# Contexts of the last block combined from SBUF, the choice of tokens marked on logits, unused products on TensorE, and six groups of weights ahead

## The chip, the core and the metric

The kernel runs on one core of one Trainium2 chip. The metric is the device time of one execution in microseconds. Times of a kernel agree within about 0.3% from run to run.

## What is computed

An image batch x of shape (4, 64, 64, 128) goes through two layers. In what follows L = 4096 is the number of tokens of an image, C = 128 the channels.

Layer 0 normalises x by groups and adds a selective scan over the tokens in three directions. Layer 1 works on the tokens of each image, and its code is what the change touches:

```python
t = t + attn(ln(t))          # q = products of cosines, 16 heads of 8 channels, softmax(q q^T / sqrt(8)) q
#   attn: x1 = ln(x + ctx @ w_comb.T + b_comb);  zf = cos(x1[:, :8]) * cos(ry)
#         ln(x1 + relu(zf @ w1.T + b1) @ w2.T + b2)
t = t + experts(ln(t))
#   experts: probs = softmax(x @ gate_w.T + gate_b, over the tokens)      64 experts
#            per expert the 8 tokens of highest probability: pooled = sum(prob * token)
#            out = gelu(pooled @ weight1 + bias) @ weight2 + bias
#            each of the 8 tokens receives prob * out
```

So each expert reads and writes 8 of the 4096 tokens of an image; the softmax over the tokens needs the logits of the whole image.

## The kernel before

Everything runs on the one core, in an order that is written out by hand: the instructions of each engine execute in the order in which the program emits them (`manual_schedule`), and pieces of work are Python generators that are stepped beside a main loop.

**Attention loop** (`loop`). For one image there are 1024 rounds: 4 sets of heads j, 8 blocks qb of 512 queries (`QB`), 32 chunks kc of 128 keys. A round computes scores on TensorE (L998), their exponential on ScalarE (L1003), and adds the values product into one PSUM bank `acc` (L1012). Row 8 of each head's 32 rows of `acc` holds the sum of the exponentials, because the values carry a column of ones. After 32 rounds `sums` copies `acc` to the tile `av` (L1021; on VectorE for the last image) and stores contexts and sums to memory (L1027, L1030, issued on POOL). For the last image (b = 3) the rounds are sorted by block (`by_block`), so the last 128 rounds are block 7 with j = 0 to 3.

In round i the program emits first the scores of round i + 1, then the step of the work beside it, then the values product of round i. For the last image the work beside is `last.turn(1.5, ...)`: each round adds a credit of 1.5 steps (at most 3 are saved), and at most one step that emits TensorE work is run in a round. A generator says that its next step is TensorE work by yielding `PE`, which `bank.take` does; beside the loop there is one PSUM bank for all of it.

**Work beside the last loop** (`last`, a chain). In this order: what is left of image 2; the experts' biases; for the image pairs (0, 1) and then (2,) `search` (logits in, the 8 highest: L1290, L1292), `choice` and `gather`; then `after` for the blocks 0 to 6 of image 3 as they become whole; then `search` of image 3 over the first seven blocks.

**The end of attention** (`after`). Per block: sums are read, inverted (L1090), stored and read back spread over the 8 channels of each head (L1102); contexts are read (L1100) and multiplied (L1107), combined with `w_comb` (co, L1115), added to the tokens, normalised (`norm`, L878 to L884, with two small operations on POOL), the cosine (Sin on ScalarE, L1226), transposed (zt, L1138), h (L1156), Relu (L1161), fo (L1169), normalised twice, transposed (xT, L1193), logits (lg, L1207, L1211).

**Choice** (`choice`). ScalarE takes the exponential of the 8 highest values (L1312) and of all logits in place (L1316), VectorE replaces the 8 highest by -1 in a copy (`match_replace`, L1320), and one pass over all 4096 columns keeps the probability where the copy is negative and zero elsewhere (L1330). `gather` then takes each group of 512 tokens: wt (chosen tokens transposed and scaled, L1342), a copy (L1348), pool (L1353), an addition (L1359), with the tokens loaded by L1337.

**Experts** (`answers`). 16 groups of 4 experts (`GE`), each with 2.1 MB of weights (L1370, L1373). Five groups are loaded ahead: one during the loop, three after it and one after the last block's logits, both on ScalarE's queue (`prefetch`). The other eleven are loaded on SP as buffers come free; two groups are in flight (`flow(..., 2, 4)`: at most two, the second four steps after the first). Then the answers go through memory (L1458, L1462), and `scatter` adds them to the tokens: 32 tiles of 512 tokens, each loaded on POOL's queue (L1440), added (L1476, L1483) and stored on SP (L1485), in a ring of `DEEP` = 12 tiles.

Of the kernel before, what the change touches and what calls it, by code (L numbers as in the profile page):

```python
# [16 lines left out]
P = 128  # L17
# [16 lines left out]
VJ = 60  # L34
QB = 512
F32R = mybir.dt.float32r


HIGH = 0xFFFFF000
# [674 lines left out]
class Attention:  # L714
# [3 lines left out]
    def __init__(self, tc, ctx, w, gate, cols, ident, bank, dram, t1, w_out, scans, sz, x):  # L718
# [52 lines left out]
        self.small = ctx.enter_context(tc.tile_pool(name="a_small", bufs=2))  # L771
        self.u, self.q, self.v, self.context, self.total, self.t2 = {}, {}, {}, {}, {}, {}
        self.xn, self.logits, self.angled, self.whole, self.closed = {}, {}, {}, {}, {}
        self.lag, self.cut = 0, False
        self.round = column(nc, const, ROUND, "round"), column(nc, const, -ROUND, "minus_round")

# [171 lines left out]
    def loop(self, b, beside, by_block=False):  # L948
# [68 lines left out]

        def sums(j, qb, i):

            av = self.mid.tile([P, QB], F32, tag="av", name=f"av_{b}_{j}_{qb}")  # L1020
            (nc.vector.tensor_copy if by_block else nc.scalar.copy)(av, accs.pop((j, qb)))  # L1021
            cut = slice(qb * QB, (qb + 1) * QB)

            def store():
                for k in range(4):
                    h = 4 * k + j
                    nc.gpsimd.dma_start(  # L1027
                        out=self.context[b][h * D : h * D + D, cut], in_=av[32 * k : 32 * k + D, :]
                    )
                nc.gpsimd.dma_start(  # L1030
                    out=self.total[b][qb].rearrange("(k j) t -> j k t", j=4)[j], in_=av[D::32, :]
                )
                if by_block and j == 3:
                    self.whole[b] = qb + 1

            later[i + 3] = store
# [22 lines left out]
    def after(self, b, gs=range(L // QB), to=None):  # L1059
# [172 lines left out]
        yield from cosines()  # L1232
        yield from flow((second(g) for g in gs), self.n, 32 // self.n)


DEEP = 12


class Experts:
# [4 lines left out]
    def __init__(self, tc, ctx, ident, weight1, weight2, block, nb):  # L1244
        nc = self.nc = tc.nc
        self.tc, self.ident, self.weight1, self.weight2, self.block, self.nb = tc, ident, weight1, weight2, block, nb
        self.const = const = ctx.enter_context(tc.tile_pool(name="e_const", bufs=1, side="right"))
        self.some = ctx.enter_context(tc.tile_pool(name="e_some", bufs=2, side="right"))
        self.bias_2 = const.tile([P, C], F32, name="bias_2")
        for k in range(2):  # L1250
            nc.scalar.dma_start(out=self.bias_2[k * E : (k + 1) * E], in_=weight2[:, FFN, :])
        self.bias_1 = const.tile([P, 4, E], F32, name="bias_1")
        self.chosen = [const.tile([P, L], F32, name=f"chosen_{j}") for j in range(nb // 2)]

        self.pooled = const.tile([P, E, 32], F32, name="pooled")
        nc.gpsimd.memset(self.pooled, 0.0)

        self.share = const.tile([P, nb // 2], F32, name="share")
        self.diagonal = const.tile([P, nb // 2, E], F32, name="diagonal")
        self.found, self.ahead, self.rooms = {}, [], 0  # L1260

    def biases(self):

# [15 lines left out]
    def search(self, images, blocks):  # L1279

        nc = self.nc
        rows = slice(images[0] % 2 * E, images[-1] % 2 * E + E)
        prob = self.const.tile([P, L], F32, tag="prob", name=f"prob_{images[0]}")
        best = self.some.tile([P, TOP + QB], F32, tag="best", bufs=1, name=f"best_{images[0]}")
        self.found[images] = rows, prob, best
        while self.block.closed[images[-1]] < blocks:
            yield WAIT
        for b in images:
            own = slice(b % 2 * E, b % 2 * E + E)
            nc.sync.dma_start(out=prob[own, : blocks * QB], in_=self.block.logits[b][:, : blocks * QB])  # L1290
        yield
        nc.vector.max(out=best[rows, :TOP], in_=prob[rows, : blocks * QB])  # L1292
        yield
# [6 lines left out]
    def choice(self, images, blocks):  # L1300

        nc, some, key = self.nc, self.some, images[0]
        rows, prob, best = self.found[images]
        top = some.tile([P, TOP], F32, tag="top", name=f"top_{key}")[rows]
        if blocks * QB < L:
            nc.vector.max(out=top, in_=best[rows, : TOP + L - blocks * QB])
        else:
            nc.vector.tensor_copy(top, best[rows, :TOP])
        low = some.tile([P, 1], F32, tag="low", name=f"low_{key}")[rows]
        nc.vector.tensor_scalar_mul(low, top[:, 0:1], -1.0)  # L1310
        yield
        nc.scalar.activation(top, top, AF.Exp, bias=low)  # L1312
        total = some.tile([P, NC], F32, tag="total", name=f"total_{key}")[rows]
        for g in range(NC):
            cut = prob[rows, g * T : (g + 1) * T]
            nc.scalar.activation(cut, cut, AF.Exp, bias=low, accum_out=total[:, g : g + 1])  # L1316
            yield

        w = self.chosen[key // 2][rows]
        nc.vector.match_replace(out=w, in_to_replace=top, in_values=prob[rows], imm_value=-1.0)  # L1320
        yield
        share = self.share[rows, key // 2 : key // 2 + 1]
        nc.vector.tensor_reduce(share, total, mybir.AxisListType.X, ALU.add)
        nc.vector.reciprocal(share, share)
        for b in images:
            own = slice(b % 2 * E, b % 2 * E + E)
            nc.vector.tensor_scalar_mul(
                self.diagonal[own, b // 2, :], self.ident[own, own], self.share[own, b // 2 : b // 2 + 1]
            )
        nc.vector.scalar_tensor_tensor(w, w, 0.0, prob[rows], ALU.is_lt, ALU.mult)  # L1330
        yield

    def pool(self, b, g):

        nc, bank, rows = self.nc, self.block.bank, slice(b % 2 * E, b % 2 * E + E)
        x = self.some.tile([P, 4, C], F32, tag="x", bufs=4, name=f"x_{b}_{g}")
        nc.sync.dma_start(out=x, in_=self.block.xn[b][:, g * 4 : g * 4 + 4, :])  # L1337
        yield
        ps = yield from bank.take(f"wt_{b}_{g}")
        for i in range(4):  # L1340
# [8 lines left out]
        bank.leave()  # L1349
        yield  # L1350
        ps = yield from bank.take(f"pool_{b}_{g}")
        for i in range(4):
            nc.tensor.matmul(ps[:, :E], x[:, i, :], wT[:, i, :], start=(i == 0), stop=(i == 3))  # L1353
        yield
        into = self.pooled[:, :, b]
        if g == 0:
# [3 lines left out]
        bank.leave()  # L1360
        yield

    def gather(self, images):
        yield from flow((self.pool(b, g) for b in images for g in range(NT // 4)), 2, 3)

    def weights(self, stream, g, by):

# [58 lines left out]
    def answers(self, ctx, out):  # L1426
        nc, tc, bank, nb = self.nc, self.tc, self.block.bank, self.nb
        once = ctx.enter_context(tc.tile_pool(name="e_once", bufs=1))
        pool = ctx.enter_context(tc.tile_pool(name="e_pool", bufs=2))
        deep = ctx.enter_context(tc.tile_pool(name="e_deep", bufs=DEEP))  # L1430
        ng = E // GE
        n = len(self.ahead)
# [12 lines left out]
        def group(g):  # L1445
            yield from self.answer(g, loaded.pop(g), o_all, pool)
            if g + n < ng:
                loaded[g + n] = self.weights(self.ahead[g % n][1], g + n, nc.sync)
            elif len(ts) < DEEP:
                bring(len(ts))  # L1450

        yield from flow((group(g) for g in range(ng)), 2, 4)
        for i in range(len(ts), DEEP):
            bring(i)
        answers = [once.tile([P, C], F32, name=f"answer_{j}") for j in range(nb // 2)]
# [66 lines left out]
def tile_kernel(tc, ctx, x, in_proj_w, dirs, out_proj_w, attn, gate, weight1, weight2, out):  # L1522
# [81 lines left out]
    scanning.close()  # L1604
    experts = Experts(tc, ctx, ident, weight1, weight2, block, nb)
    experts.prefetch(experts.room(ctx, 1, "right"), nc.gpsimd)
    blocks = L // QB
    pairs = [(b, b + 1) for b in range(0, nb - 2, 2)] + [(nb - 2,), (nb - 1,)]
    with tc.manual_schedule():
# [4 lines left out]
                for part in (experts.search(images, blocks), experts.choice(images, blocks), experts.gather(images))  # L1614
            ),
            block.after(nb - 1, range(0, 4)), block.after(nb - 1, range(4, 6)), block.after(nb - 1, range(6, blocks - 1)),
            experts.search(pairs[-1], blocks - 1),
        )
        block.loop(nb - 1, lambda i: last.turn(1.5, i % 3 > 0 or i > 830), True)
        last.rest()  # L1620
        block.cut = False
    loop.close()
    with ExitStack() as end:
        block.bank = Bank(end.enter_context(tc.tile_pool(name="end_ps", bufs=7, space=PSUM)), 7)
        with tc.manual_schedule():
            room = experts.room(end, 3)
            with ExitStack() as pieces:
                block.pieces_of(pieces, 1, opening=False)
                closing = block.after(nb - 1, range(blocks - 1, blocks), experts.rest(pairs[-1], blocks - 1))
                for i, _ in enumerate(closing):  # L1630
                    if i == 2:
                        experts.prefetch(room, nc.scalar)
            experts.prefetch(experts.room(end, 1), nc.scalar)
            for _ in experts.choice(pairs[-1], blocks - 1):
                pass
            for _ in experts.gather(pairs[-1]):
                pass
            for _ in experts.answers(end, out):
                pass

# [31 lines left out]
```

## Time and profile before

| | us |
|---|---|
| median of three runs | 11418.36 (11410.22 to 11421.47) |
| the profiled execution, its own time | 11412.32 |
| its span | 11410.5 |
| TensorE busy in the span | 9874.3 (87%) |
| ScalarE busy | 9993.7 (88%) |
| VectorE busy | 8258.3 (72%) |
| last product of the attention loop ends | 11161.9 |
| co of the last block starts | 11187.6 |
| its lg starts | 11226.1 |
| first wt of the last image starts | 11246.4 |
| first product of the experts starts | 11281.9 |
| last copy of the experts' outputs ends | 11355.3 |
| first product of scatter starts | 11364.6 |

The lower rows come from the timeline of the profiled execution, which lists the instructions of every engine with their start and duration. Of the 249 us after the attention loop each engine is busy for a part only. In the page's slices of the span TensorE's granted clock is full in most of the attention loops; behind the last one it is half for long stretches.

### The profile page before, as it was taken

How to read it: one execution, taken by the hardware profiler on the slowest of the kernel's cores; microseconds unless marked ns; L12 is line 12 of the kernel's file. 1: busy time of each engine (PE TensorE's matmuls, PEld its weight loads, DVE VectorE, ACT ScalarE, POOL GpSimd, SP SyncE). 2: the span in 40 equal slices, each digit the busy share in tenths (PEclk: the TensorE clock that was granted, in tenths of full speed). 3: DMA queues.
4: the chain of work that ended last, by engine and by line, in shares of the span. 5: the costliest groups of instructions: out<-in, count | busy, mean ns of one | idle time of the engine just before them, and what ended most of it. 6: DMA issues, size and time to landing. Idle time of an engine off the chain costs nothing.

```text
span 11410.5 us, 183033 instructions
## 1 busy us (share of the span) xinstructions
PE 9874.3 (87%) x68358; PEld 3273.6 (29%) x68358; DVE 8258.3 (72%) x8405; ACT 9993.7 (88%) x10828; POOL 3790.3 (33%) x3891
## 2 busy tenths in 40 slices
PE   6687792788998889899998899999998999999995
PEld 2233331222222222222222222222222223333323
DVE  6889997888888987999988979988998321111212
ACT  4566672899999999999999999999999999989992
POOL 4777784332323223424333124243331110000000
PEclk8798895899999999999999999999999999999997
DMA  6778897656565665665656755656556332222225
GB/s 188 226 231 230 226 249 198 161 145 156 142 155 155 178 174 146 158 154 142 151 147 160 194 157 156 156 141 151 146 147 162 116 100 72 76 71 84 75 65 186
DMA packets 900980, 1747.52 MB, mean 153 GB/s; under 512 B 203150, under 2 KB 443846, under 8 KB 899830
## 3 DMA queue, kind: packets, MB, share of 16 engines
q1 hardware_dynamic: 764734, 1469.68, 47.9%
q0 software_dynamic: 93856, 156.41, 4.8%
q10 hardware_dynamic: 41496, 109.71, 3.6%
q8 instruction: 537, 8.80, 0.3%
q14 instruction: 357, 2.92, 0.1%
HBM read 1379.76 MB, written 355.47 MB: 152 GB/s over the span
## 4 chain that ended last, share of the span: by engine, by line
PE 38%; ACT 24%; issue 14%; DVE 11%; DMA 10%; POOL 1%; SPq 1%; ACTq 0%; DVEq 0%; POOLq 0%
PE acc L1012 21%; ACT e L1003 20%; PE s L998 10%; DVE h L561 5%; DMA delta<-d_delta 4%; PE cv L412 2%; DMA du<-d_du 2%; DVE dB L551 1%; ACT dA L542 1%; PE y L599 1%; ACT delta L542 1%; PE fo L1169 1%; PE xd L426 1%; PE h L1156 1%; DMA w<-in_L_ffn_weight_dram 1%
## 5 line engine op out<-in xcount | busy, mean ns | idle before, releaser
L1003 ACT ACTIVATE e<-s 128x1024 f32<-128x1024 f32 x8192 | 7778.1, 1105 | 234.2 <-PE s L998 222.2
L1012 PE MATMUL acc<-e,val 128*32 128x512 f32 x32768 | 5250.2, 615 | 106.5 <-ACT av L1021 93.7
L998 PE MATMUL s<-qm,key 32*128 32x512 f32 x16384 | 2650.8, 501 | 588.8 <-ACT e L1003 558.9
L998 PEld LDWEIGHTS s<-qm,key 32*128 32x128 f32 x16384 | 1013.4, 184 | 4444.4 <-issue 2483.9
L563 POOL COPY ends<-h 128x1 f32<-128x1 f32 x1152 | 1333.8, 1159 | 2362.4 <-DVE h L561 2353.2
L551 DVE TENSOR_TENSOR dB<-du,B 128x1024 f32<-128x1024 f32 x960 | 1213.6, 1264 | 441.2 <-PE y L599 217.2
L1012 PEld LDWEIGHTS acc<-e,val 128*32 128x32 f32 x32768 | 973.5, 109 | 1608.4 <-issue 789.0
L561 DVE TENSOR_TENSOR_SCAN h<-dA,ends,dB 128x1024 f32<-128x1024 f32 x576 | 1351.2, 2346 | 110.3 <-ACT dA L542 66.2
L542 ACT ACTIVATE dA<-delta,A 128x1024 f32<-128x1024 f32 x768 | 935.7, 1218 | 500.5 <-DMA delta<-d_delta 460.8
L561 DVE TENSOR_TENSOR_SCAN h<-delta,ends,du 128x1024 f32<-128x1024 f32 x432 | 1013.2, 2345 | 127.2 <-ACT delta L542 64.3
L568 POOL TENSOR_TENSOR hC<-h,C 128x1024 f32<-128x1024 f32 x384 | 993.5, 2588 | 153.3 <-PE y L599 83.7
L542 ACT ACTIVATE delta<-delta,A 128x1024 f32<-128x1024 f32 x768 | 937.4, 1221 | 7.3 <-DVE dB L551 2.2
L572 DVE TENSOR_TENSOR du<-h,C 128x1024 f32<-128x1024 f32 x576 | 702.2, 1219 | 0.1
L572 DVE TENSOR_TENSOR dB<-h,C 128x1024 f32<-128x1024 f32 x576 | 702.2, 1219 | 0.0
L551 DVE TENSOR_TENSOR du<-du,B 128x1024 f32<-128x1024 f32 x576 | 691.6, 1201 | 5.8 <-DMA B<-d_bc 5.8
L1027 POOL DMA_DIRECT2D d_ctx<-av x512 | 260.3, 518 | 1026.1 <-DVE av L1021 647.6
L412 PE MATMUL cv<-xn,conv 128*128 128x512 f32 x1024 | 469.7, 612 | 26.8 <-DVE xn L346 17.2
L593 POOL DMA_DIRECT2D d_du<-x_delta x272 | 157.2, 578 | 1003.0 <-DVE x_delta L592 945.1
L561 DVE TENSOR_TENSOR_SCAN h<-dA,dB 128x1024 f32<-128x1024 f32 x192 | 438.9, 2286 | 50.3 <-ACT dA L542 40.9
L599 PE MATMUL y<-hC,sel 128*32 128x256 f32 x3072 | 247.8, 456 | 171.7 <-DVE o L615 160.0
L599 PE MATMUL y<-dB,sel 128*32 128x256 f32 x4608 | 378.8, 401 | 9.9 <-DVE xT L1196 4.8
L561 DVE TENSOR_TENSOR_SCAN h<-delta,du 128x1024 f32<-128x1024 f32 x144 | 329.1, 2285 | 68.3 <-issue 35.0
(246 smaller groups left out, 7200.5 us busy)
## 6 DMA issues: line engine op xcount, KB each, us to landing
delta<-d_delta SPq DMA_DIRECT2D x768, 512.0 KB
du<-d_du SPq DMA_DIRECT2D x576, 512.0 KB
du<-d_du ACTq DMA_DIRECT2D x192, 512.0 KB
key<-d_q SPq DMA_DIRECT2D x352, 256.0 KB
d_u<-u SPq DMA_DIRECT2D x48, 1024.0 KB
d_delta<-r SPq DMA_DIRECT2D x48, 1024.0 KB
B<-d_bc SPq DMA_DIRECT2D x96, 512.0 KB
C<-d_bc SPq DMA_DIRECT2D x96, 512.0 KB
```

The costliest lines, as they stand in the source:

```text
L412: nc.tensor.matmul(banks[2 * m + g], w["conv"][:, k, m * P : (m + 1) * P], reads(k, g), start=(k == 0), stop=(k == 3))
L542: nc.scalar.activation(tiles["delta", s], t, AF.Exp, scale=A)
L551: nc.vector.tensor_mul(tiles["du", s], du, spread[order, c, "B", j % 2])
L561: nc.vector.tensor_tensor_scan(h, dA, dB, first, ALU.mult, ALU.add)
L563: nc.gpsimd.tensor_copy(ends[order, c][:, at : at + 1], h[:, T - 1 :])
L568: nc.gpsimd.tensor_mul(tiles["du", s], h, spread[order, c, "C", j % 2])
L572: nc.vector.tensor_mul(dB, h, spread[order, c, "C", j % 2])
L599: nc.tensor.matmul(y[32 * g : 32 * g + 32, : T // 4], self.sel[:, j // 2, :], hC[:, 256 * g : 256 * g + 256], start=(j == 0), stop=(j == 3),)
L998: nc.tensor.matmul(s_ps[:, k, :], keys[f"{i // 4}"][rows, cut].bitcast(F32R), queries[j, qb][rows, :].bitcast(F32R), start=True, stop=True,)
L1003: nc.scalar.activation(e, s_ps, AF.Exp, scale=1.0 / math.sqrt(D))
L1012: nc.tensor.matmul(accs[j, qb][32 * k : 32 * k + 32, :], v[:, k * VW : k * VW + 32], es[i][k // 2][:, k % 2, :], start=(kc == 0), stop=(kc ...
L1027: nc.gpsimd.dma_start(out=self.context[b][h * D : h * D + D, cut], in_=av[32 * k : 32 * k + D, :])
```

## The change

The diff, cut to its core (lines that only move a pool or rename a slice are left out):

```diff
@@ Attention.loop, sums
-            av = self.mid.tile([P, QB], F32, tag="av", name=f"av_{b}_{j}_{qb}")
+            av = self.mid.tile([P, QB], F32, tag="av", bufs=4, name=f"av_{b}_{j}_{qb}")
             (nc.vector.tensor_copy if by_block else nc.scalar.copy)(av, accs.pop((j, qb)))
+            if by_block and qb == L // QB - 1:
+                self.kept[j] = av
+                return
@@ Attention, new
+    def combs(self, pool, some, w_comb):
+        self.comb = pool.tile([P, 4, C], F32, name="comb")
+        raw = some.tile([P, C], F32, tag="wT", name="raw_comb_by_head")
+        nc.sync.dma_start(out=raw, in_=w_comb)
+        spaced = some.tile([P, 4, C], F32, tag="x", bufs=4, name="comb_by_head")
+        nc.gpsimd.memset(spaced, 0.0)
+        yield
+        by_j = raw.rearrange("o (k j d) -> j o k d", j=4, d=D)
+        for j in range(4):
+            nc.vector.tensor_copy(spaced[:, j, :].rearrange("o (k r) -> o k r", r=32)[:, :, :D], by_j[j])
+        yield
+        for pair in range(2):
+            ps = yield from self.bank.take(f"comb_{pair}")
+            for j in range(2):
+                nc.tensor.transpose(ps[:, j * C : (j + 1) * C], spaced[:, 2 * pair + j, :], self.ident)
+            yield
+            nc.vector.tensor_copy(self.comb[:, 2 * pair : 2 * pair + 2, :]..., ps[:, : 2 * C])
+            self.bank.leave()
+        yield
+    def divide(self, j):
+        while j not in self.kept:
+            yield WAIT
+        av = self.kept[j]
+        r = self.piece([P, QB], "p0", name=f"part_{j}")
+        halves = [slice(i * QB // 2, (i + 1) * QB // 2) for i in range(2)]
+        ps = yield from self.bank.take(f"whole_{j}")
+        for i, cut in enumerate(halves):
+            if i:
+                yield from self.pause()
+            for k in range(4):
+                rows = slice(32 * k, 32 * k + 32)
+                one = self.ident[:, 32 * k + D : 32 * k + D + 1].to_broadcast([P, 32])
+                nc.tensor.matmul(ps[rows, cut], one, av[:, cut], start=True, stop=True)
+        yield
+        for cut in halves:
+            nc.vector.reciprocal(r[:, cut], ps[:, cut])
+            nc.vector.tensor_mul(av[:, cut], av[:, cut], r[:, cut])
+        self.bank.leave()
+        yield
+    def warm(self, n, by):
+        for i in range(n):
+            self.nc.tensor.matmul(self.spare, self.ident, by, start=True, stop=True)
+    def ending(self, b, to, by, prefetch):
...
+        nc.sync.dma_start(out=u, in_=self.u[b][:, cut, :])
+        nc.sync.dma_start(out=t, in_=self.t1[b].rearrange("(t p) c -> p t c", p=P)[:, cut, :])
+        yield from self.divide(3)
+        prefetch()
+        nc.vector.tensor_add(u, u, spread("b_comb"))
+        for k in range(4):
+            for j in range(4):
+                nc.tensor.matmul(ps[:, at], self.kept[j][:, at], self.comb[:, j, :], start=(j == 0), stop=(j == 3))
+        self.warm(8, by)
...
+        nc.scalar.activation(z, z, AF.Sin, bias=self.half_pi, scale=-1.0)
...
+                    nc.tensor.matmul(ps[:, k * C : (k + 1) * C], h[:, f, at], self.w2[:, f, :], ...)
+        self.warm(9, by)
...
+        nc.tensor.matmul(ps[rows], self.gate, xT, start=True, stop=True)
+        self.warm(12, by)
...
@@
-DEEP = 12
+DEEP = 8
@@ Experts.choice
-        nc.scalar.activation(top, top, AF.Exp, bias=low)
+        w = self.chosen[key // 2][rows]
         for g in range(NC):
-            nc.scalar.activation(cut, cut, AF.Exp, bias=low, accum_out=total[:, g : g + 1])
+            nc.scalar.activation(w[:, cut], prob[rows, cut], AF.Exp, bias=low, accum_out=total[:, g : g + 1])
             yield
-        nc.vector.match_replace(out=w, in_to_replace=top, in_values=prob[rows], imm_value=-1.0)
+        nc.vector.match_replace(out=prob[rows], in_to_replace=top, in_values=prob[rows], imm_value=GONE)
...
-        nc.vector.scalar_tensor_tensor(w, w, 0.0, prob[rows], ALU.is_lt, ALU.mult)
+    def marks(self, images, g):
+        cut = slice(g * QB, (g + 1) * QB)
+        w = self.chosen[images[0] // 2][rows, cut]
+        self.nc.vector.scalar_tensor_tensor(w, prob[rows, cut], 0.9 * GONE, w, ALU.is_lt, ALU.mult)
@@ Experts.pool
+        if b == images[0]:
+            self.marks(images, g)
+        if not ahead:
+            self.tokens(b, g)
         yield
@@ Experts.answers
-        pool = ctx.enter_context(tc.tile_pool(name="e_pool", bufs=2))
+        pool = ctx.enter_context(tc.tile_pool(name="e_pool", bufs=3))
-        yield from flow((group(g) for g in range(ng)), 2, 4)
+        yield from flow((group(g) for g in range(ng)), 3, 2)
@@ tile_kernel
-            experts.search(pairs[-1], blocks - 1),
+            experts.search(pairs[-1], blocks - 1), block.combs(experts.const, experts.some, attn["w_comb"]),
+            *(block.divide(j) for j in range(3)),
...
-            experts.prefetch(experts.room(end, 1), nc.scalar)
+            experts.prefetch(experts.room(end, 2), nc.scalar)
+            for g in range(4):
+                experts.tokens(nb - 1, g)
             for _ in experts.choice(pairs[-1], blocks - 1):
                 pass
-            for _ in experts.gather(pairs[-1]):
+            for _ in experts.gather(pairs[-1], 4):
                 pass
+            logits.close()
```

In words. The four `av` tiles of the last block stay in SBUF (`kept`). `divide` spreads the row of sums over the 32 rows of each head with products against columns of the identity, inverts and multiplies in place; the parts j = 0 to 2 are divided beside the loop, the last one behind it. `combs`, beside the loop and after the last `search`, lays `w_comb` out so that four products per 128 tokens, one for each j, combine the contexts. `ending` takes the place of `after` for the last block: nothing of it goes through memory, h and lg are computed in calls of 512 columns, the eight channels of the cosine are scaled before the others, b2 is added before fo. `warm` emits 8, 9 and 12 products of 128x128 by 128x512 that nobody reads, behind co, behind fo and behind lg. In `choice` the exponentials go to the tile of chosen weights while the 8 highest logits are overwritten with a very low number, and `marks` clears the weights of the others by groups of 512 columns, at the first step of each `pool`. Six groups of weights are loaded ahead, the last two behind the last block's logits; four groups of tokens of the last image are loaded ahead of its choice; three groups of experts are in flight; the ring of `scatter` has 8 tiles. The logits' tiles have a pool of their own, which is closed before `answers` opens its pools.

## Prediction

> **What bounds the kernel now.** The change touches the attention loop of the last image and the end behind it, so I read these two from the trace. All stamps below are us from the start of the span. First, who waited for whom on TensorE from 11160 to the end of the span (columns: total us, times, longest):
>
> ```profile
> PE co L1115 <- DVE cT L1107: 25.7, 1, 25.7
> PE wt L1342 <- DVE chosen L1330: 18.4, 1, 18.4
> ```
>
> The end is a chain, not a loaded engine: TensorE stands still while the last block's contexts go through memory and back (co), and while the choice of the last image is made (wt). The timeline says the loop's last product ends at 11161.90, and co starts at 11187.58.
>
> Second, the choice of earlier images inside the loop. In the timeline (start, us, engine, line, tile), around the first of them:
>
> ```profile
> 10035.29 4.43 DVE L1330 SCALAR_TENSOR_TENSOR chosen<-chosen,prob 128x4096 f32<-128x4096 f32 x1
> 10039.77 1.96 PE L1342 MATMUL wt<-diagonal,chosen 64*128 64x64 f32 x8 [4.63 <-DVE chosen L1330]
> 10044.42 1.94 ACT L1003 ACTIVATE e<-s 128x1024 f32<-128x1024 f32 x2 [7.16 <-PE s L998]
> ```
>
> TensorE waits for one VectorE pass over 4096 columns; the loop's own products stand behind it, and the exponentials of ScalarE, which bound this loop (99.5% busy at 10500 to 10700), lose 7.16 us. The other choice does the same at 10239.87, with 6.83 us lost.
>
> Third, the tail of the block before the last one, where the change puts its preparation of the weights (comb):
>
> ```profile
> 11027.94 0.65 PE L1207 MATMUL lg<-xT,gate 128*64 128x256 f32 x2
> ...
> 11032.05 0.49 SPq L1290 DMA_DIRECT2D prob<-d_lg  x1
> ...
> 11039.77 3.89 DVE L1292 MAX8 best<-prob 64x8 f32<-64x3584 f32 x1 [10.39 <-DMA prob<-d_lg]
> ```
>
> VectorE is held by this load and MAX8 until 11043.66.
>
> Fourth, stages with their busy times, granted clock (third from the end), DMA share and GB/s:
>
> ```profile
> 11164.00:11168.00 4.00, 0.00 (x0) 0.00 (x0) 0.00 (x0) 0.00 (x0) 1.49 (x3) 0.87 1.03 378
> 11246.00:11282.00 36.00, 31.01 (x132) 28.55 (x136) 5.82 (x17) 0.00 (x0) 0.00 (x0) 0.50 0.10 30
> 11311.00:11330.00 19.00, 12.89 (x221) 6.78 (x218) 4.63 (x9) 5.74 (x10) 0.00 (x0) 1.00 1.05 386
> ```
>
> TensorE's clock falls within 6 us of the loop's end; the gather (second line) runs its whole 36 us at half clock; the expert stage (third) is bound by the transfers of weights.
>
> **What the Trainium skill says.** "TensorE: Matmul & The Clock Gate", section "What's actually happening": the clock is half or full, decided over free-running windows of about 3.4 us. The trace agrees: falls at 11166.96 and 11218.2, rises at 11211.3 and 11289.8, computed from the clock of 4 us stretches, lie whole multiples of 3.41 us apart. The same page, "Step-by-step: what each phase is for": matmuls stay in program order, which is the 4.63 us above. "VectorE: DVE Perf Modes", "First, the fixed hardware budget": reciprocal repeats a divide step eight times; the trace has 1.74 us for a reciprocal of 128x256 against 0.42 us for an addition of that size. "DMA: Bandwidth & Descriptors", "Issuing engines are not separate DMA queues": all queues share the same 16 engines; the trace shows one stage full at 386 GB/s.
>
> **The change part by part.** A minus is time won.
>
> 1. *Marks instead of a full pass, in the loop.* The pass of 4.43 us before the first wt becomes one mark of 512 columns, 0.70 us (4.42/8 plus the 0.15 us of the smallest VectorE rows). First choice: marks end at 10035.96, wt takes 1.03 at full clock, the next products 1.0 and 0.5, so ScalarE resumes near 10038.65 after its last exponential at 10037.26: 1.4 us lost instead of 7.16 and a following 0.66. With the dropped exponential of the top values (0.2): -6.6. Second: 1.1 instead of 6.83, and 0.1: -5.8. Sum **-12.4**. The seven later marks of each image (0.70 us) lie on VectorE, under 30% busy there, two paced steps ahead of their products.
>
> 2. *comb, in the loop.* After the lg product at 11027.94 the hand-paced order counts seven steps to comb's first transposes: lgs, the prob load, MAX8, load and memset, four copies, take, transposes. At 1.5 steps a round (3 at most saved up) that is four or five rounds later. The products of those rounds start at 11035.36 and 11037.19; so there TensorE reaches the transposes. The four copies stand behind MAX8 on VectorE (the 64 KB load is issued on SP right behind prob, and the memset runs on POOL, which is idle there, so neither is later): 11043.66 + 4 x 0.22 = 11044.5. TensorE waits 7.4 to 9.2 us, its products queued behind. ScalarE has work for about 2.3 us more, then resumes 3.3 us after TensorE does (0.5 transposes, 1.9 and 0.7 cold products, 0.2), as it did at 10044.42; with the 0.66 of a second cold round, **+10**. Bounds: 0, if the copies were somehow done before TensorE arrives, and +11.
>
> 3. *divide of three parts, in the loop.* Each is 8 column-tiled calls over 256 columns, two steps of 0.5 us on TensorE (8 instructions over 512 take 1.0). A round without filler has 0.4 us of slack (1.84 us against 0.43 + 1.0), so they are nearly free: **+0.5**. Without the slack they cost 3. VectorE's 4.4 us each lie after the copy of acc, not ahead of it.
>
> 4. *From the loop's end (0 = 11161.90) to the cosine.* Removed: stores of contexts and sums, the load of sums, reciprocal, store and load of shares, multiply. Now: copy av to 0.7, first half of the sums on TensorE to 1.4, then reciprocal and product twice (1.74 + 0.42 + small change, 4.45): 5.9. co is 32 instructions instead of 8; three of four parts of each quarter don't wait, so most runs before 5.9 and it ends at about 8.0 (3.9 us of instructions at the 0.12 us that wt has at full clock; 7.0 at half). Add b_comb is hidden under co if u has landed: a load of 32 KB took 5.3 us beside the weights, so u at 5 to 6. After 0.8 for the sum, norm takes 4.25 and seven small rows 1.55: z at 14.6. ScalarE must first issue the loads of three groups; before, its Sin table came at 16.5 to 17.7, behind waiting issues. With sums and shares gone from these queues I take 15.3 (bounds 14.6 and 17.7). The cosine began at 36.0: **-20.7**.
>
> 5. *Cosine to the logits.* Eight unused products stand behind co on TensorE. No row shows one; h, 128x256 columns at half clock, took 7.19/16 = 0.45 us an instruction, so 512 columns twice take 0.9 at full and 1.8 at half clock: 7.2 or 14.4 us. From 8.0 they end at 15.2, just ahead of the cosine, or up to 7 late if the clock fell before; I charge +1. Then zt at full clock -0.45, h with a part at full clock -2.5 (0 to -3.4), b2 now hidden under h -0.6, fo as before. Nine products (8.1 us) end before the 11.1 us that fo's end and xT lie apart. xT and lg -1.2. Sum with fo's +0.3: **-3.4**, between +3 and -7.
>
> 6. *Choice of the last image.* wt came 18.4 us after lg. The pass becomes a mark, -3.7, the exponential of the top values goes, -0.2. But ScalarE issues two groups ahead of its table load, not one: five issues took 2.66 us, and ten took 8.67 in the first prefetch, where issues waited. Between 5.3 and 8.7, that is +2.6 to +6.0, middle 4.5: **+0.7**. Twelve products last 10.8 to some 13 us and end under this.
>
> 7. *Gather.* They end more than 3.4 us before wt, so the clock falls again; and 36 us of gather did not raise it before. Marks lie beside TensorE's 4.4 us an iteration. **-0.3**.
>
> 8. *Experts.* Ten groups are streamed, not eleven: 2.1 MB at 386 GB/s, -5.4. With three groups in flight two more products precede the first o at half clock, so its buffer, and the transfers behind it, come 2.4 us later (7.3 to 9.7): **-3.1**, between 0 and -6.
>
> 9. *Scatter.* Eight tiles instead of twelve are there when it starts: four more loads, 1.05 MB at 330 to 350 GB/s, +3.1, with all engines full from 11368 on. A shorter ring adds bubbles: **+4**, between +2 and +8. The tiles' early loads, on POOL, now wait for the logits' buffer and fall into the gather, where DMA is idle.
>
> Sum: -12.4 + 10 + 0.5 - 20.7 - 3.4 + 0.7 - 0.3 - 3.1 + 4 = **-24.7 us**. The profiled execution took 11412.3 us (span 11410.5 and 1.8 around it), so it would take 11387.6; it lay 6.0 below the median of the three runs, 11418.36. On the median: **11393.7, say 11394**. About 0.2%, 22.8 us, is what a measurement can tell from no change; the forecast sits just beyond it.
>
> **Rivals.**
> - *comb's transposes don't wait*: part 2 costs nothing, 11384. For it: the paced steps could fall later than I count. Against: VectorE is visibly held to 11043.66.
> - *The gather keeps full clock*: eight iterations of 2.5 instead of 4.4 us, -15: 11379. For it: the twelve products before it. Against: they end early, and the gather itself did not warm TensorE.
> - *The new covers are too short*: products at half clock delay zt by 7, ScalarE's issues take the upper ends (+2.4 at the cosine, +1.5 at the choice), h stays cold (+2.5): 13 less gain, 11407. For it: the fall to half clock at 11166.96, just where co will run. In effect the change does only half of what it says.
> - *Slower: scatter bound by turns of its ring.* Place: the last stage. A buffer's turn (load, add, store, next load) took 15.4 us on the chain with twelve. If it doesn't shorten with eight, 24 tiles need 46 us and the stage grows by about 10, not 4. It turns the result slower from +28.7, a turn of some 21 us; at 23 us (69 + 6 against 41: +34) the result is 11424. Against it: turns were long because the engines were full, and fewer transfers in flight shorten them.
>
> **How the numbers follow.** Forecast 0.60 (its own range 11384 to 11403), no comb wait 0.13, warm gather 0.10, short covers 0.13, slower 0.04. The range 11376 to 11408 takes in the two faster cases' centres and the short covers. Faster by over 0.2% (below 11395.6): 0.35 of the forecast's 0.60, nearly all of the next two, 0.57 together; within: 0.39; slower 0.04.
>
> **What would show it.** Waits of TensorE for the first marks near 1 us at two places, and no loss of 7 us on ScalarE there; one new wait of 7 to 9 us for the copies of comb; the cosine 15 us after the last acc, not 36; clock 1.0 at zt but 0.5 in the gather; ten groups on SP; scatter some 4 us longer. I am wrong if comb's wait is missing, the gather runs at full clock, or ScalarE's issues hold up cosine and exponentials by more than 6 us.

## The result, and the profile after

| | before | after |
|---|---|---|
| median, us (13 runs each) | 11410.22 (11399.97 to 11428.21) | 11384.86 (11368.63 to 11400.75) |
| profiled execution / its span | 11412.32 / 11410.5 | 11400.64 / 11398.9 |
| last image's loop, first to last exponential | 2034.4 | 2027.4 |
| last acc (the loop's last values product) to the end of the span | 248.7 | 235.4 |

The ratio is 0.9976 (95%: 0.9969 to 0.9983): 25 us less by the medians, 19 to 35 by the interval. The profiled execution of the changed kernel lies 15.8 us above its median. It entered the last image's loop 8.7 us later than the kernel before did, behind code whose only edit is more buffers for av; from there on it won 7.0 + 13.3 us. So stages are compared from their own starts, not by stamps.

Who waited for whom on TensorE, 9300 us to the end, after (total us, times, longest; lines of the experts, of scatter and of waits that hardly changed are left out):

```profile
PE comb L1256 <- DVE comb_by_head L1251: 7.8, 1, 7.8
PE wt L1489 <- DVE chosen L1470: 7.0, 3, 5.6
PE whole L1277 <- DVE part L1280: 2.8, 1, 2.8
PE co L1309 <- DVE av L1281: 1.5, 1, 1.5
```

The 25.7 us of co are 1.5 now, and the wait for the choice is down to 5.6 at the end. Two waits in the loop are new: comb's, and one of divide's products for divide's own reciprocals. The timeline of after (start, us, engine, line) shows three places: the first choice, comb, the cosine.

```profile
10040.46 0.69 DVE L1470 SCALAR_TENSOR_TENSOR chosen<-prob,chosen 128x512 f32<-128x512 f32 x1
10041.21 1.10 PE L1489 MATMUL wt<-diagonal,chosen 64*128 64x64 f32 x8 [0.90 <-DVE chosen L1470]
10043.84 3.77 ACT L1005 ACTIVATE e<-s 128x1024 f32<-128x1024 f32 x4 [1.41 <-PE s L1000]
...
11028.71 3.89 DVE L1427 MAX8 best<-prob 64x8 f32<-64x3584 f32 x1 [9.73 <-DMA prob<-d_lg]
11032.63 0.44 DVE L1251 COPY comb_by_head<-raw_comb_by_head 128x32 f32<-128x32 f32 x4
11032.87 0.69 PE L1256 MATMUL comb<-ident,comb_by_head 128*128 128x128 f32 x2 [7.84 <-DVE comb_by_head L1251]
11036.25 11.11 ACT L1005 ACTIVATE e<-s 128x1024 f32<-128x1024 f32 x12 [9.09 <-PE s L1000]
...
11164.07 8.80 ACTq L1523 DMA_DIRECT2D w<-in_L_ffn_weight_dram  x4
...
11176.45 3.59 ACTq L1523 DMA_DIRECT2D w<-in_L_ffn_weight_dram  x4
11180.08 1.28 ACT L1320 ACT_TABLE_LOAD   x1 [17.62 <-DMA w<-in_L_ffn_weight_dram]
11181.37 0.32 ACT L1320 ACTIVATE z<-z,a_half_pi 128x32 f32<-128x32 f32 x1
```

This choice costs ScalarE 1.41 us instead of 7.16; comb costs it 9.09. In the third part the cosine's argument is ready at 11177.9, but ScalarE loads Sin's table only when its last issue of weights is through, so the cosine runs 17.8 us after the last acc. Stages of after (clock third from the end, then DMA share and GB/s): beside co, gather, experts, scatter.

```profile
11166.00:11170.00 4.00, 2.39 (x20) 2.01 (x18) 3.93 (x5) 0.00 (x0) 0.00 (x0) 1.00 1.04 386
11228.00:11263.00 35.00, 30.86 (x128) 28.36 (x128) 10.08 (x22) 0.00 (x0) 4.32 (x8) 0.50 0.19 58
11309.00:11328.00 19.00, 12.79 (x195) 7.28 (x184) 4.22 (x10) 4.58 (x8) 0.00 (x0) 0.81 0.96 356
11345.00:11399.00 54.00, 27.40 (x256) 25.39 (x256) 21.58 (x33) 0.00 (x0) 13.11 (x24) 0.59 0.90 273
```

The gather is still at half clock, and scatter takes 54 us at 273 GB/s, where the kernel before took 45.9.

### The profile page after: what moved, and what is told of

Read it like the earlier page. It is cut to its first block, busy times and chain, and to the rows that moved or that the text cites. A ratio compares the mean times of both kernels' runs of the same rounds, so it can differ in the third digit from the quotient of the medians.

```text
span 11398.9 us, 183299 instructions
## 1 busy us (share of the span) xinstructions
PE 9915.1 (87%) x68498; PEld 3286.5 (29%) x68498; DVE 8296.0 (73%) x8444; ACT 9992.4 (88%) x10825; POOL 3738.2 (33%) x3870
## 4 chain that ended last, share of the span: by engine, by line
PE 37%; ACT 24%; issue 14%; DVE 13%; DMA 10%; POOL 1%; SPq 1%; ACTq 0%; DVEq 0%; POOLq 0%
PE acc L1014 20%; ACT e L1005 20%; PE s L1000 10%; DVE h L562 6%; DMA delta<-d_delta 4%; PE cv L413 2%; DVE dB L552 2%; DMA du<-d_du 1%; ACT dA L543 1%; ACT delta L543 1%; PE y L600 1%; PE fo L1174 1%; PE h L1161 1%; PE xd L427 1%; DVE du L573 1%
## 5 line engine op out<-in xcount | busy, mean ns | idle before, releaser
L564 POOL COPY ends<-h 128x1 f32<-128x1 f32 x1152 | 1294.3, 1124 | 2404.1 <-DVE h L562 2394.5
L51 POOL TENSOR_TENSOR rs_x<-mv_x,eps 128x4 f32<-128x4 f32 x96 | 94.3, 983 | 918.8 <-DVE mv_x L881 918.7
```

What stands on the lines that cost most here:

```text
L564: nc.gpsimd.tensor_copy(ends[order, c][:, at : at + 1], h[:, T - 1 :])
```

## Experiments

My theory was the sum of the prediction; the rivals are named with each run. Medians are set against the runs of the kernel before on the same chip, and stages come from each kernel's own profile. Of the chips used here the changed kernel ran only on the one where the kernel before has the median 11417.47; on the others it is placed by its ratio of 0.9977.

**The changed kernel again** (no edit).

> The changed kernel itself once more, unaltered, because its parts as traced add up to less than the medians moved: in the first profile of it the end (last acc to the end of the span) won 13.3 us and the last image's loop 7.0, while 8.7 us were lost before that loop, where nothing was changed. Theory 1 (the 8.7 us are chance, the end is as traced): the end takes 235 us again (233 to 238), the last loop some 2027, the start of the last loop lies anywhere between 9125 and 9136, and the median is 20 to 28 us below the kernel before. Theory 2 (the end was unlucky in that one profile): the end takes 225 us or less this time, with the gather at full clock or the scatter near 46 us.

Measured: 11390.17 against 11417.47, ratio 0.9977 (0.9969 to 0.9984). The last loop began at 9124.3 and took 2031.2, the end 231.9. Gather 35.4 at half clock, scatter 50.6. The 8.7 us ahead of the loop are within chance: over the twelve profiles of this study, which differ little in what is ahead of it, this start lies between 9111.6 and 9143.2. The end fell between the figures of the two theories (233 to 238, and 225 or less): an unlucky end explains 3.5 us, and scatter alone took 3.4 less.

The length of the loop scatters too. Six of the profiles have the loop of after, and it took 2027.2 to 2034.5 us in them. In all twelve ScalarE is busy for 1926 to 1927 us of it, so what differs is its idle time, and that can be read by stretches. From 800 to 1250 us into the loop, where the two choices lie, it is idle for 44.6 us before and 32.1 to 32.6 in the six; in the last 160 us, where comb and divide lie, for 4.6 before and 14.2 to 16.1 in the six.

**Marks alone**, in the kernel before.

```diff
-            cut = prob[rows, g * T : (g + 1) * T]
-            nc.scalar.activation(cut, cut, AF.Exp, bias=low, accum_out=...)
+            nc.scalar.activation(w[:, cut], prob[rows, cut], AF.Exp, bias=low, accum_out=...)
-        nc.vector.match_replace(out=w, ..., imm_value=-1.0)
+        nc.vector.match_replace(out=prob[rows], ..., imm_value=GONE)
-        nc.vector.scalar_tensor_tensor(w, w, 0.0, prob[rows], ALU.is_lt, ALU.mult)
+        if b == images[0]:
+            self.marks(images, g)      # in pool: 512 columns, ahead of wt
```

> The kernel before with only the marks: exponentials written straight into chosen, match_replace writing a mark into prob, and one pass of 512 columns ahead of each group of products instead of one of 4096 behind match_replace; no comb, no divide, the end as before. Theory 1 (part 1 of the prediction): both losses of ScalarE of 7.16 and 6.83 us fall to 1.4 and 1.1, the last loop is 12 to 13 us shorter, the choice at the end 3.7 to 3.9 us (lg to wt 14.5 to 14.7), in all -16 us. Rival (the products are held by something else next, such as diagonal or the load of tokens): TensorE waits 4 us or more at wt still, loop gains under 5 us.

Measured: 11395.09 against 11417.47, ratio 0.9982 (0.9975 to 0.9990). Timeline of this kernel at its first choice:

```profile
10053.35 1.10 PE L1349 MATMUL wt<-diagonal,chosen 64*128 64x64 f32 x8 [0.90 <-DVE chosen L1336]
10055.98 4.69 ACT L1004 ACTIVATE e<-s 128x1024 f32<-128x1024 f32 x5 [1.41 <-PE s L999]
```

ScalarE loses 1.41 us here and 1.05 at the second choice; lg to wt takes 14.4 (before 18.4), the loop 2019.2. From 800 to 1250 us into the loop ScalarE is idle for 32.4 us, as in after. The rival falls. This one edit gives 22 us by the medians, more than the 16 expected, where the whole change gives 27 on this chip.

**Everything but the marks**: the same diff taken back in the changed kernel.

> The changed kernel without its marks: the pass of 4096 columns is back, the exponentials are written into prob again; all else as changed. With marks alone the kernel before won some 20 us by its trace. Theory 1 (the parts add up: marks 12.4 in the loop and 3.9 at the end, all the rest +12 in the loop and -9 to -13 at the end): the last loop takes 2042 to 2048 us, the end 235 to 239, and the time lies within 10 us of the kernel before, that is, the rest of the change is worth next to nothing. Rival (the rest is worth as much as the marks, and the two overlap): 15 us or more below the kernel before.

Measured: 11405.31 against 11411.88, ratio 0.9994 (0.9985 to 1.0002); last loop 2043.6, end 233.8. The rest of the change is not told from nothing. By the trace it wins 14.8 us behind the loop and pays 9.2 in it. With the old pass ScalarE's idle time around the two choices is back at 45.5 us.

**comb early.** It goes to the head of the work beside the last loop, and each divide is followed by six empty steps.

```diff
-            last.parts, experts.biases(),
+            last.parts, experts.biases(), block.combs(experts.const, experts.some, attn["w_comb"]),
...
-            experts.search(pairs[-1], blocks - 1), block.combs(experts.const, experts.some, attn["w_comb"]),
+            experts.search(pairs[-1], blocks - 1),
@@ divide
-        yield
+        for _ in range(1 if j == 3 else 6):
+            yield
```

> The preparation of comb is moved to the start of the last image's loop, and six empty paced steps follow each divide there, so that the bank is free again before the next one. Theory 1 (part 2 of the prediction: the transposes cost because they stand in front of the loop's products while VectorE is held by the load and MAX8; and divide(1) waits for the reciprocals of divide(0) on the single bank): the wait of 7.84 us for comb_by_head and ScalarE's gap of 9.09 us go, so does the gap of 2.75 us; the last loop is 11 to 12 us shorter than the changed kernel's 2027, and the time 9 to 13 below it. Rival (the loop was due to lose this time anyway, or the transposes wait as long at the other place): 0 to -3 us.

Measured: 11384.77 against 11417.47, ratio 0.9970 (0.9959 to 0.9982): 5 below the changed kernel on that chip, where 9 to 13 were expected; last loop 2022.2. Six runs can't tell 5 from 9 with certainty, but the trace shows that the gain is missing: in the last 160 us of the loop ScalarE is idle for 14.2 us, as in the lowest of the six with comb in its old place. Both waits are gone, but ScalarE has a new gap of 9.57. Timeline of this kernel there:

```profile
11010.85 3.89 DVE L1428 MAX8 best<-prob 64x8 f32<-64x3584 f32 x1 [9.74 <-DMA prob<-d_lg]
11014.77 1.76 DVE L1280 RECIPROCAL part<-whole 128x256 f32<-128x256 f32 x1
...
11018.69 0.43 DVE L1281 TENSOR_TENSOR av<-av,part 128x256 f32<-128x256 f32 x1
11019.04 0.68 DVE L1023 COPY av<-acc 128x512 f32<-128x512 f32 x1
11019.78 1.94 PE L1014 MATMUL acc<-e,val 128*32 128x512 f32 x8 [8.94 <-DVE av L1023]
```

The line to read is the copy of acc: it became due near 11010.8 and stood behind MAX8 and the whole of divide(0), 8.2 us. So the theory was too narrow. Not comb is the cost, but whatever TensorE needs from VectorE just while the search holds it. It had to be tried with that queue kept clear:

```diff
+    def copied(self, j):
+        while j not in self.kept:
+            yield WAIT
@@ beside the last loop, with comb early as above
-            experts.search(pairs[-1], blocks - 1), *(block.divide(j) for j in range(3)),
+            block.copied(1), block.divide(0), experts.search(pairs[-1], blocks - 1), block.divide(1), block.divide(2),
```

> The changed kernel with comb prepared at the start of the loop, and with the first divide and the search of the last image (its load and MAX8) held until the next acc has been copied (kept holds part 1); six empty paced steps behind each divide. In the earlier try comb's wait went, but acc then waited 8.9 us for the copy of av, which stood on VectorE behind MAX8 and the two halves of divide(0). Theory 1 (VectorE's queue ahead of the copy of acc is the cost, whatever is put there): neither wait is left, the last loop takes 2019 to 2022 us, as with marks alone (2019.2), and the time falls 9 to 13 us below the changed kernel. Rival (the loop loses its 9 us at some third place, because the paced steps are due by then): the last loop stays at 2027 or more.

Measured: 11371.69 against 11414.36, ratio 0.9966 (0.9953 to 0.9978); last loop 2010.5, shorter than expected. In its last 160 us ScalarE is idle for 3.9 us (before 4.6): what comb and divide cost is gone. From 10990 to the loop's end TensorE waits for VectorE 2.5 us in all:

```profile
PE xT L1198 <- DVE x1r L886: 2.1, 1, 2.1
PE whole L1282 <- DVE av L1023: 0.4, 1, 0.4
```

The loop is even shorter than with marks alone (2019.2). Of the 20 us against the mean of the six (2030.4), 11 lie in the last 160 us. The rest is spread over gaps earlier in the loop. Moving comb to the head moves every paced step behind it; whether that is the reason was not tried.

**Without unused products** (`warm(8)`, `warm(9)`, `warm(12)` become `warm(0)`).

> The changed kernel without its unused products (none behind co, fo and lg), which leaves no result out. Theory 1 (they buy next to nothing: h, lg and the gather run at half clock with them too): acc to the cosine and the gather unchanged within 0.5 us, cosine to the end of lg 28.4 to 30.5, the time within 3 us of the changed kernel. Rival (they hold the clock up through zt and part of fo and lg): cosine to lg longer by 3 to 5 us, the time by as much.

Measured: 11383.79 against 11414.36, ratio 0.9976 (0.9967 to 0.9984); last acc to cosine 18.25, cosine to the end of lg 30.05, gather 35.44. As placed, they are worth some 1.3 us (cosine to the end of lg 28.8 in the mean of four profiles with them) and can't be seen in the time.

**More of them** (12, 9 and 18), and one in each iteration of the gather.

```diff
+        if ahead:
+            self.block.warm(1, self.chosen[0][:, :512])
         yield
         ps = yield from bank.take(f"pool_{b}_{g}")
```

> The changed kernel with 12, 9 and 18 unused products instead of 8, 9 and 12, and one more in each iteration of the gather between wt and pool: an unused product of 128x512 took 0.86 to 0.88 us at full clock. Theory 1 (the clock falls because TensorE stands still for some us ahead of h and of the gather, and with that filled it stays): h at full clock, cosine to lg 24.5 to 26 instead of 28.4; the gather at clock 1.0 takes 25 to 28 us instead of 35.4; in all 10 to 14 us less. Rival (products of few rows or columns do not count, so the clock falls all the same): clock 0.5 in the gather, each iteration 1.75 us longer, the gather 45 to 50 us, the time 10 to 14 us more.

Measured: 11372.42 against 11414.36, ratio 0.9967 (0.9954 to 0.9979). The gather takes 25.4 us instead of 35.4, cosine to lg 26.2, since h now starts at full clock and takes 4.38 us (7.19 in after). The end takes 214.5 us, 18 less than the mean of after's (232.5), where 10 to 14 were expected. The gather's window, and two stretches near its start:

```profile
11219.00:11244.00 25.00, 24.93 (x144) 19.49 (x144) 10.12 (x22) 0.00 (x0) 2.93 (x6) 0.93 0.20 60
11220.00:11224.00 4.00, 4.00 (x16) 2.78 (x15) 1.39 (x3) 0.00 (x0) 0.00 (x0) 0.57 0.00 0
11224.00:11228.00 4.00, 4.00 (x26) 3.18 (x26) 1.71 (x4) 0.00 (x0) 0.00 (x0) 1.00 0.36 89
```

TensorE has more to do than in the gather of after and is done 10 us sooner: clock 0.93 in place of 0.50. The rival falls. The clock even fell at the start of this gather (0.57) and rose again inside it, which it never does in the gather of after.

**Weights issued by SP.**

```diff
-                    lambda: experts.prefetch(room, nc.scalar),
+                    lambda: experts.prefetch(room, nc.sync),
-            experts.prefetch(experts.room(end, 2), nc.scalar)
             for g in range(4):
                 experts.tokens(nb - 1, g)
+            experts.prefetch(experts.room(end, 2), nc.sync)
```

> The changed kernel with the weights of groups 1 to 5 issued by SP instead of ScalarE, the first four loads of tokens ahead of the last two groups. Theory 1 (ScalarE's issues hold up its loads of tables for Sin and Exp): last acc to the cosine 14.3 to 15.0 us instead of 17.3 to 18.7, end of lg to wt 14.5 to 15 instead of 18.1, the time 6 to 8 us less. Rival (the loads of u and t or of the tokens get behind the weights on SP, or land later because the weights start sooner): the cosine at 16 or more, or wt held by tokens; under 3 us gained.

Measured: 11370.42 against 11414.36, ratio 0.9965 (0.9953 to 0.9978). The end takes 215.7 us, some 17 less than the mean of after's, where 6 to 8 were expected. Timeline of this kernel:

```profile
11149.91 1.28 ACT L1320 ACT_TABLE_LOAD   x1
11165.35 0.32 ACT L1320 ACTIVATE z<-z,a_half_pi 128x32 f32<-128x32 f32 x1 [14.16 <-DVE z L126]
11167.35 3.70 PE L1332 MATMUL h<-zT,w 8*128 8x512 f32 x8 [1.02 <-DVE zT L1327]
11171.78 1.28 ACT L1451 ACT_TABLE_LOAD   x1
11192.98 1.14 ACT L1451 ACTIVATE chosen<-prob,low 64x1024 f32<-64x1024 f32 x1 [19.91 <-DVE low L1445]
```

Both table loads now lie far ahead of their users: the cosine waits for its argument (DVE z) and starts 14.35 us after the last acc, the exponentials wait for the maximum. lg to wt takes 12.85 instead of 18.1, more than I gave it, since Exp's table load left the path as well. h ran at full clock (3.70 us; 7.19 in after). The twelve unused products now reach to wt, and the gather shows that this alone is not enough:

```profile
11203.00:11207.00 4.00, 3.27 (x25) 2.90 (x24) 1.64 (x4) 0.00 (x0) 0.00 (x0) 1.00 0.06 22
11207.00:11235.00 28.00, 24.39 (x106) 22.42 (x104) 8.69 (x19) 0.00 (x0) 4.31 (x8) 0.53 0.24 78
```

It starts at full clock and is at half some 5 us later: a mean of 0.53 over 28 us leaves full clock less than 2 of them. The products inside each iteration are what held it before. The last run below has the same products ahead and one in each iteration, and keeps 1.00. Whether it is the gaps they fill or the size of these products that counts was not tried apart.

**DEEP = 12** in the changed kernel, six groups ahead.

> DEEP back to 12 in the changed kernel, six groups of weights still ahead. Theory 1 (scatter lost through its shorter ring, four loads that are not there at its start and bubbles behind stores): scatter goes from 54.0 us back to 46 to 47, the expert stage stays within 1.5 us, the time falls by 6 to 8 us against the changed kernel. Theory 2 (only the four loads' bytes were moved, from the expert stage to the scatter): scatter gains 3 to 4 us and the expert stage gives back as much, no change in time. Theory 3 (the expert stage's transfers collide with four more early loads): expert stage up by over 3 us.

Measured: 11384.21 against 11417.47, ratio 0.9970 (0.9959 to 0.9982). Scatter:

```profile
11325.00:11371.00 46.00, 23.66 (x256) 21.58 (x254) 21.18 (x32) 0.00 (x0) 10.92 (x20) 0.65 0.94 297
```

46.2 us, as before the change (45.9), and the experts give nothing back (68.5; 72.2 and 70.4 in the two profiles of after). Theories 2 and 3 fall. The end takes 223.7 us, 8.8 less than the mean of after's; the medians say 6 with six runs.

**All that paid, together**: comb early with the copy kept clear, SP's issues, DEEP 12, one unused product in each iteration of the gather.

> The changed kernel with what has paid in single runs put together: comb early and VectorE's queue kept clear ahead of the copy of acc; weights issued by SP; DEEP 12; one unused product in each iteration of the gather. Theory 1 (different stages, so they add up, but for the fills of the gather, which b_on_sp had in part): last loop 2010 to 2022 us; end: 14.4 + 25.3 + 12.9 + 25.5 + 67 + 9.5 + 46 = 200 us, against 232 to 235; the time 45 to 55 us below the changed kernel, some 0.993 of the kernel before. Rival (with the covers and ScalarE's issues gone the expert stage gets the transfers that were early before, and gives 10 us or more back there): the end at 210 or more.

Measured: 11348.54 against 11411.88, ratio 0.9943 (0.9931 to 0.9956): 63 us below the kernel before and some 37 below the changed one, less than the 45 to 55 expected. The profiled execution was the shortest of five, 11338.85; in it the last loop takes 2013.1, the end 199.8. These two are 50 us below their means in the changed kernel; why the medians show 13 less stays open. The end is where the sum put it, and the rival, that the experts would give back 10 us, falls (69 us):

```profile
11190.00:11213.00 23.00, 23.00 (x143) 18.07 (x142) 10.12 (x22) 0.00 (x0) 3.00 (x6) 1.00 0.22 67
11213.00:11282.00 69.00, 47.94 (x705) 26.07 (x704) 15.76 (x33) 20.41 (x33) 3.48 (x7) 0.89 0.93 344
11292.00:11337.00 45.00, 24.35 (x256) 21.73 (x255) 21.39 (x33) 0.00 (x0) 10.92 (x20) 0.65 0.94 304
```

## Why the prediction was right, step by step

The forecast was 24.7 us less; the medians say 25.4. For the end the table has the mean of four profiles that share it (after, again, comb early, after the copy); for the loop, single gaps of after.

| step of the prediction | predicted | traced |
|---|---|---|
| 1 marks in the loop | -12.4 | -12.4 |
| 2 comb | +10 | +9.1 |
| 3 divide | +0.5 | +2.75 |
| 4 last acc to the cosine | -20.7 | -17.8 (36.0 to 18.3) |
| 5 cosine to lg | -3.4 | -1.4 (30.2 to 28.8) |
| 6 choice | +0.7 | -0.3 |
| 7 gather | -0.3 | 0.0 |
| 8 experts, to the first sc | -3.1 | -3.0 (82.7 to 79.7) |
| 9 scatter | +4 | +6.2 (45.9 to 52.1) |
| sum | -24.7 | -16.9 |

*Step 1.* From the end of the last exponential ahead of the first choice to ScalarE's resume behind the second it took 207.2 us before and 194.8 after: 12.4. Marks alone and everything but the marks confirm it from both sides: idle time around the choices 32.4 and 45.5 us.

*Step 2* was right in place, cause and size: TensorE waited 7.84 us and ScalarE lost 9.09. What I had not seen is that taking comb away wins hardly anything there as long as VectorE's queue is held there: then the copy of acc meets the search and the divide behind it, and ScalarE loses 9.57.

*Step 3* is mis-sized. "VectorE's 4.4 us each lie after the copy of acc, not ahead of it" held, but divide(1) followed divide(0) at once and its products had to wait 2.78 us for the reciprocals still reading the one bank; ScalarE lost 2.75. With six empty steps between them the wait is gone.

*Step 4* took 15.3 for the cosine, with 17.7 as the bound; all four profiles lie beyond that bound, at 17.8 to 18.7. "With sums and shares gone from these queues" the issues did not get shorter: the last ended at 11180.0, 16.5 us after the last acc, just as before. The argument was ready at 11177.9, 14.3 us after the last acc, as worked out (14.6). The run with SP put the cosine at 14.35. "ScalarE: Activation LUTs", section "What ACT_TABLE_LOAD costs", in the Trainium skill gives the load 1283 ns, which is the 1.28 us of every trace here; the drain of 1380 ns that it adds is not seen: Sin starts 0.01 us behind the load at 11180.08.

*Step 5.* The unused products were not late, as I feared with +1, but h stayed cold (7.19 us), so the 2.5 for a part at full clock did not come. *Step 6* came out 1.0 below the middle: the ten issues took 6.3 us, 3.7 more than five did. (The middle of +2.6 and +6.0 is 4.3, not 4.5, so the step should have said +0.4.)

*Step 8* has the right sum for the wrong reason, and that is luck. The first group's o was to end 2.4 us later (9.7 after the first product of the experts, not 7.3); it ended at 7.2 to 7.7 in the four profiles, so nothing was lost there. The group that is no longer streamed was to win 5.4, and the stage won 3.0; what took the rest is not traced.

*Step 9* is the largest miss within its bounds. Four loads more, +3.1, I had; the rest, put at 1 for bubbles, is 3. In the list of waits over scatter VectorE waits for loads of t 14.6 us before, 25.2 after, and 15.0 with DEEP = 12, which takes the whole loss back. The stores show the turns: the 1st, 9th, 17th and 25th tile are stored 2.8, 13.1, 25.5 and 38.6 us after scatter's first product, so a turn of eight tiles takes 10 to 13 us; with twelve, before, it took 12.7 and 16.0. So the rival that turns of the ring bind scatter had the mechanism; the turns got shorter, but not in step with the ring, and the size is +6, not +10.

So the mechanisms held in the main, but that 24.7 met 25.4 so closely is in part luck. The traced steps give 17, not 25; the loop as a whole moved by -4.0 (mean 2030.4 of six kernels with it unchanged from after, one profile before), the end by -16.2, together 20, which the interval (19 to 35) holds at its edge. In the loop the difference from the single gaps (-0.6) lies inside its own scatter of 7 us. My misses in 4, 5 and 9 (7 us) were made good by something that I can't name. Whether the code ahead of the last loop became some us faster, with four buffers for av, stays open: a start that scatters over 30 us can't show it in a few profiles.

The rival of a gather at full clock fell. Of the two reasons given, that the products end too early was not what decided it: in the run with SP's issues they reach to wt, and the clock falls all the same. That the gather itself doesn't keep TensorE warm held. The rival of covers too short was half true (cosine and h as it said, no late products).

## What to carry to other kernels

Ahead of a paced insertion ask not only what the inserted step waits for, but what stands on each in-order queue when the main loop next needs it: a VectorE held for 8 us, by a search that waits for its load or by the divide behind it, cost ScalarE 9 us through comb, and through the copy of acc when comb was gone. DMA issues on ScalarE are work on ScalarE, and a table load behind them waits until the last is through; SP had room for them. Unused products paid most inside the slow stretch (10 us in the gather); ahead of h, four more of them went with some 2.6 us less in one profile. And when a change has nine parts, take the likeliest alone first: one of them had 22 of the 27 us.

## What the runs showed that I had not expected

- A gather in which TensorE is busy for 30.86 of 35 us by its records stays at clock 0.50; one product of 128x512 in each iteration keeps it at 0.93 to 1.00. Records that look dense did not keep the clock up here.
- ScalarE loads a table as soon as it reaches the instruction, 20 us ahead of its use if nothing stands before it: with the issues on SP, Exp's load ran at 11171.78, its first use at 11192.98.
- Four issues of weights took ScalarE 8.80 us from the first to the last, and 2.15 and 3.59 the next two times. Each issue by itself took 0.33 to 0.75 us; the rest are pauses between issues, two of 1.7 and 5.4 us in the first four, beside a DMA that was full (386 GB/s from 11166 to 11170). What a pause waits for is not shown.
